# Attention over convolved features: q's tile ordered by form, then by block of n

The change makes the moving operand of an energy one piece of 1024 bytes, where it was two pieces of 512.

## Chip, cores and metric

One core of a Trainium2 chip runs the kernel. The metric is the device time of one execution in microseconds (us), lower is better; the runs of one kernel on one chip lay within 0.16% of one another here (31 of the kernel before on chip 0: 2494.62 to 2498.60 us). Kernels that are compared ran on one chip in the same rounds. Ratios are the mean time of one kernel's fast runs over that of the other's of the same rounds, so not quite the ratio of the medians that are quoted.

## The reference, cut to what matters

```python
# x: (4, 64, 64, 256) float32; Wq, Wk: 256 x 128; Wv: 256 x 256
q = einsum('bwhc,cd->bwhd', x, Wq) + bq     # k, v likewise
pq, pk, pv = (t.reshape(B, -1, N) for t in (q, k, v))          # N = 4096
energy = einsum('bcn,bcm->bnm', pq, pk)     # contraction over 128
attention = softmax(energy, axis=-1)
out = einsum('bcm,bnm->bcn', pv, attention).reshape(B, W, H, C)
return gamma * out + x
```

## The kernel before

Every float32 factor is cut into parts, so that three matmuls stand for one product: q and k each have three forms (f = 0, 1, 2). One image is 16 groups of 256 columns n; a group is 8 steps. A step makes the energies of four blocks of m, three steps ahead, and multiplies four blocks of finished weights by v. TensorE's program of a step is therefore 12 energies (sa, sa, sb, four times), then 8 matmuls with vh, 8 with vl, both into the banks `a`, and 8 with vd into `bb`. Each has a weight load of 128 columns ahead of it.

```python
def halved(f, x):
    h = f[:, :, 0, :]
    nc.scalar.activation(h, x, AF.Identity, scale=UPPER / 64)
    for j, s, op in ((1, -64.0, ALU.add), (2, 64.0 * (1.0 + E), ALU.subtract)):
        nc.vector.scalar_tensor_tensor(f[:, :, j, :], h.bitcast(F32), s, x, ALU.mult, op)

def halve_q(b, g):                                  # once in a group of 8 steps
    t = work.tile([P, NJ, 3, P], F32R, tag="q", name=f"q_{b}_{g}")     # NJ = 2
    halved(t, loads.pop((b, "qr", g)))
    loads[b, "q", g] = t

def energy(b, u, k):                                # twice in a step
    ...
    sa = ps_s.tile([P, 2, NJ, P], F32, tag="a", ...)      # one PSUM bank, of two
    sb = ps_s.tile([P, 2, NJ, P], F32, tag="b", ...)
    for i in range(2):
        for to, f, first, last in ((sa, 0, True, False), (sa, 1, False, True), (sb, 2, True, True)):
            nc.tensor.matmul(                       # out, weights (stationary), moving operand
                to[:, i], kt[:, 2 * k + i, f, :], q[:, :, f, :], start=first, stop=last
            )
    # ScalarE: exp of sa into x, then of sb into y; later VectorE: x = x*y

def attend(b, u):
    ...
    for left, right in ((h, vh), (l, vl), (d, vd)):
        for j in range(NJ):
            out_ = bb[:, j, :] if left is d else acc[j]
            for i in range(4):
                m = 2 * t + i // 2 + NI * (i % 2)
                nc.tensor.matmul(out_, left[:, i, j * P : (j + 1) * P], right[:, m, : out_.shape[1]], ...)
```

## Time and profile before

| | before |
|---|---|
| time, median of the first 3 runs | 2496.63 us (2496.11 to 2496.65) |
| TensorE, VectorE, ScalarE busy | 99%, 84%, 72% of the span |
| energies: matmuls, time from their starts to the next start | 6144, 746 us |
| granted TensorE clock | 0.999 |

The lines of the profile are shown in the prediction below. In a line of a group, the columns are the source line, the engine, the operation, output<-input, sizes and count, then the busy time in us and the mean duration of one in ns, then the engine's idle time in front. In a view by order of time, the columns are the start and the length in us and the number of instructions merged (x8). Durations of matmuls overlap (an energy's record lasts 283 ns in the mean, and the next one starts some 117 ns later), so I use the **pitch**: the time from one start to the next. Pitches to the nanosecond, in the tables, are worked out from the starts of the single records in each trace: of energies followed by an energy (and of bb followed by a matmul of attend or a transpose), with gaps of 150 ns and more, which are waits, counted apart.

### The profile page before, as it was taken

How to read it: one execution, taken by the hardware profiler on the slowest of the kernel's cores; microseconds unless marked ns; L12 is line 12 of the kernel's file. 1: busy time of each engine (PE TensorE's matmuls, PEld its weight loads, DVE VectorE, ACT ScalarE, POOL GpSimd, SP SyncE). 2: the span in 40 equal slices, each digit the busy share in tenths (PEclk: the TensorE clock that was granted, in tenths of full speed). 3: DMA queues.
4: the chain of work that ended last, by engine and by line, in shares of the span. 5: the costliest groups of instructions: out<-in, count | busy, mean ns of one | idle time of the engine just before them, and what ended most of it. 6: DMA issues, size and time to landing. Idle time of an engine off the chain costs nothing.

```text
span 2494.1 us, 50085 instructions
## 1 busy us (share of the span) xinstructions
PE 2480.4 (99%) x19982; PEld 2438.2 (98%) x19982; DVE 2106.5 (84%) x2440; ACT 1806.0 (72%) x3138; POOL 424.4 (17%) x780
## 2 busy tenths in 40 slices
PE   9999999999999999999999999999999999999998
PEld 8999999999899999999989999999998999999998
DVE  5888888888698888888869888888886988888887
ACT  5777777777677777777667777777766777777775
POOL 4211111111411111111041111111114111111110
PEclk9999999999999999999999999999999999999999
DMA  7766666665776666666477666666648666666663
GB/s 230 221 198 207 204 200 196 202 199 157 232 224 190 207 202 201 205 188 207 143 244 223 196 194 209 201 207 197 191 145 253 218 201 196 202 202 208 199 193 109
DMA packets 137408, 498.92 MB, mean 200 GB/s; under 512 B 15536, under 2 KB 57264, under 8 KB 137168
## 3 DMA queue, kind: packets, MB, share of 16 engines
q0 software_dynamic: 92320, 453.17, 58.4%
q1 hardware_dynamic: 44304, 42.22, 5.7%
q8 instruction: 160, 2.62, 0.4%
q14 instruction: 80, 0.66, 0.1%
q10 hardware_dynamic: 544, 0.26, 0.0%
HBM read 445.25 MB, written 50.33 MB: 199 GB/s over the span
## 4 chain that ended last, share of the span: by engine, by line
PE 97%; ACT 2%; DVE 1%; issue 0%; DMA 0%; SPq 0%; ACTq 0%; DVEq 0%
PE a L370 38%; PE sa L320 19%; PE bb L370 18%; PE sb L320 10%; PE qk L136 5%; PE v L157 4%; PE xt L123 1%; PE ot L416 1%; ACT h L339 1%; DVE x L334 1%; ACT x L324 0%; ACT y L324 0%; DMA x<-in_x_dram 0%; DVE vd L287 0%; ACT vh L284 0%
## 5 line engine op out<-in xcount | busy, mean ns | idle before, releaser
L324 ACT ACTIVATE x<-sa 128x512 f32<-128x512 f32 x1024 | 608.2, 594 | 400.7 <-PE sa L320 324.7
L320 PE MATMUL sa<-q,k 128*128 128x256 f32 x4096 | 757.2, 283 | 0.8 <-ACT x L324 0.8
L334 DVE TENSOR_TENSOR x<-x,y 128x1024 f32<-128x1024 f32 x512 | 625.2, 1221 | 155.6 <-ACT y L324 155.6
L320 PEld LDWEIGHTS sa<-q,k 128*128 128x128 f32 x4096 | 625.7, 189 | 2.2 <-ACT x L324 1.6
L345 DVE TENSOR_TENSOR l<-x,h 128x1024 fp32r<-128x1024 f32 x512 | 623.2, 1217 | 0.0
L348 DVE SCALAR_TENSOR_TENSOR d<-h,x 128x1024 fp32r<-128x1024 f32 x512 | 623.1, 1217 | 0.0
L324 ACT ACTIVATE y<-sb 128x512 f32<-128x512 f32 x1024 | 612.9, 599 | 0.0
L320 PE MATMUL sb<-q,k 128*128 128x256 f32 x2048 | 581.9, 284 | 0.0
L370 PE MATMUL a<-vh,h 128*128 128x258 f32 x4096 | 578.4, 284 | 0.0
L339 ACT ACTIVATE h<-x 128x1024 fp32r<-128x1024 f32 x512 | 543.3, 1061 | 42.7 <-DVE x L334 38.2
L370 PE MATMUL a<-vl,l 128*128 128x258 f32 x4096 | 573.3, 282 | 0.0
L370 PE MATMUL bb<-vd,d 128*128 128x256 f32 x4096 | 557.3, 278 | 0.0
L304 POOL DMA_DIRECT2D k<-kf x512 | 279.6, 546 | 1486.7 <-PE sb L320 1468.1
L370 PEld LDWEIGHTS a<-vh,h 128*128 128x128 f32 x4096 | 526.5, 190 | 0.0
L370 PEld LDWEIGHTS a<-vl,l 128*128 128x128 f32 x4096 | 526.2, 190 | 0.0
L370 PEld LDWEIGHTS bb<-vd,d 128*128 128x128 f32 x4096 | 514.1, 188 | 0.0
L320 PEld LDWEIGHTS sb<-q,k 128*128 128x128 f32 x2048 | 384.6, 188 | 8.9 <-ACT y L324 0.8
L136 PE MATMUL qk<-wqk_sb,xts 128*128 128x256 f32 x512 | 122.5, 382 | 0.0
L400 DVE SCALAR_TENSOR_TENSOR o<-a,o 128x256 f32<-128x256 f32 x126 | 47.6, 419 | 86.8 <-ACT o L380 86.8
L157 PE MATMUL v<-xts,wv_sb 128*128 128x256 f32 x512 | 120.3, 379 | 0.0
L157 PEld LDWEIGHTS v<-xts,wv_sb 128*128 128x128 f32 x512 | 97.3, 190 | 13.2
L408 ACT ACTIVATE o<-o,r 128x256 f32<-128x256 f32 x126 | 57.4, 502 | 72.3 <-DVE r L391 72.3
(54 smaller groups left out, 929.4 us busy)
## 6 DMA issues: line engine op xcount, KB each, us to landing
k<-kf POOLq DMA_DIRECT2D x512, 768.0 KB, 4.8
x<-in_x_dram SPq DMA_DIRECT2D x128, 256.0 KB, 3.7
kf<-f POOLq DMA_DIRECT2D x64, 384.0 KB, 4.0
out_dram<-x POOLq DMA_DIRECT2D x63, 256.0 KB, 2.5
qd<-qks POOLq DMA_DIRECT2D x128, 64.0 KB, 3.1
qr<-qd SPq DMA_DIRECT2D x64, 128.0 KB, 3.0
wv_sb<-in_L_conv_Wv_dram POOLq DMA_DIRECT2D x1, 256.0 KB, 6.2
out_dram<-x SPq DMA_DIRECT2D x1, 256.0 KB, 4.0
```

The source lines that it names most:

```text
L136: nc.tensor.matmul(qk[:, s, :], self.xt[i][:, k, s, :], wqk_sb[:, k, :], start=(k == 0), stop=(k == KC - 1),)
L157: nc.tensor.matmul(vp[:, eh, :], wv_sb[:, k, eh * P : (eh + 1) * P], self.xt[i][:, k].rearrange("p s a -> p (s a)"), start=(k == 0), stop= ...
L304: nc.gpsimd.dma_start(t.rearrange("p (i s) f d -> p i s (f d)", s=2), kf[b, u % NU])
L320: nc.tensor.matmul(to[:, i], kt[:, 2 * k + i, f, :], q[:, :, f, :], start=first, stop=last)
L324: nc.scalar.activation(to[:, 2 * k : 2 * k + 2, :], sp.rearrange("p i j d -> p i (j d)"), AF.Exp, scale=scale,)
L334: nc.vector.tensor_tensor(x, x, y, ALU.mult)
L339: nc.scalar.activation(h, units[b, u], AF.Identity, scale=UPPER)
L345: nc.vector.tensor_tensor(l, x, h.bitcast(F32), ALU.subtract)
L348: nc.vector.scalar_tensor_tensor(d, h.bitcast(F32), 1.0 + E, x, ALU.mult, ALU.subtract)
L370: nc.tensor.matmul(out_, left[:, i, j * P : (j + 1) * P], right[:, m, : out_.shape[1]], start=(t == i == 0 and (left is h or left is d and ...
L400: nc.vector.scalar_tensor_tensor(o[:, j, :], a[:, :C], 1.0 + E, o[:, j, :], ALU.mult, ALU.add)
L408: nc.scalar.activation(o[:, j, :], o[:, j, :], AF.Identity, scale=r[:, j : j + 1])
```

## The change

The intent is that the stream of an energy runs over one contiguous piece. The tile is ordered (form, block, element) in place of (block, form, element); its size, its writers and the matmuls are the same.

```diff
         def halve_q(b, g):
-            t = work.tile([P, NJ, 3, P], F32R, tag="q", name=f"q_{b}_{g}")
-            halved(t, loads.pop((b, "qr", g)))
+            t = work.tile([P, 3, NJ, P], F32R, tag="q", name=f"q_{b}_{g}")
+            halved(t.rearrange("p f j d -> p j f d"), loads.pop((b, "qr", g)))
@@ energy
-                        to[:, i], kt[:, 2 * k + i, f, :], q[:, :, f, :], start=first, stop=last
+                        to[:, i], kt[:, 2 * k + i, f, :], q[:, f], start=first, stop=last
```

## The prediction

> **What bounds the kernel now.** I read the page's busy table first, then the chain that ended last, then the groups, then the order of time of one step of the main loop, and last the records of single matmuls in the trace.
>
> ```profile
> PE 2480.4 (99%) x19982; PEld 2438.2 (98%) x19982; DVE 2106.5 (84%) x2440; ACT 1806.0 (72%) x3138; POOL 424.4 (17%) x780
> ...
> PE 97%; ACT 2%; DVE 1%; issue 0%; DMA 0%; SPq 0%; ACTq 0%; DVEq 0%
> PE a L370 38%; PE sa L320 19%; PE bb L370 18%; PE sb L320 10%; PE qk L136 5%; PE v L157 4%; PE xt L123 1%; PE ot L416 1%; ACT h L339 1%; DVE x L334 1%; ACT x L324 0%; ACT y L324 0%; DMA x<-in_x_dram 0%; DVE vd L287 0%; ACT vh L284 0%
> ```
>
> TensorE is the bound: it is 97% of the chain, and the energies (sa and sb, L320, the only matmuls that read q) are 29% of it, some 720 us. VectorE at 84% and ScalarE at 72% have slack. A busy TensorE need not run at its best rate, so what counts is the time from one matmul's start to the next, which I call pitch. The groups show that the energies are not out of line in duration:
>
> ```profile
> L320 PE MATMUL sa<-q,k 128*128 128x256 f32 x4096 | 757.2, 283 | 0.8 <-ACT x L324 0.8
> L320 PE MATMUL sb<-q,k 128*128 128x256 f32 x2048 | 581.9, 284 | 0.0
> L370 PE MATMUL a<-vl,l 128*128 128x258 f32 x4096 | 573.3, 282 | 0.0
> L370 PE MATMUL bb<-vd,d 128*128 128x256 f32 x4096 | 557.3, 278 | 0.0
> ```
>
> The bb group is the comparison to use: 256 columns too, but its moving operand vd is already one piece of 1024 bytes. An energy reads q in two pieces of 512 bytes, 1536 bytes apart. Here are a bb block and an ordinary energy block in order of time (start, length, then the instruction):
>
> ```profile
> 1005.64 1.08 PE L370 MATMUL bb<-vd,d 128*128 128x256 f32 x8
> 1006.56 0.40 PE L320 MATMUL sa<-q,k 128*128 128x256 f32 x2
> 1006.79 0.28 PE L320 MATMUL sb<-q,k 128*128 128x256 f32 x1
> ...
> 1007.85 0.28 PE L320 MATMUL sb<-q,k 128*128 128x256 f32 x1
> 1007.97 0.33 PE L370 MATMUL a<-vh,h 128*128 128x258 f32 x1
> ```
>
> Eight bb take 1006.56 - 1005.64 = 0.92 us, 115 ns each; the twelve energies take 1007.97 - 1006.56 = 1.41 us, 117.5 ns each. Now the step that follows the output transposes, once in a group of eight steps:
>
> ```profile
> 1014.80 1.11 PE L370 MATMUL bb<-vd,d 128*128 128x256 f32 x8
> 1015.75 0.40 PE L320 MATMUL sa<-q,k 128*128 128x256 f32 x2
> ...
> 1017.02 0.28 PE L320 MATMUL sb<-q,k 128*128 128x256 f32 x1
> 1017.13 0.28 PE L370 MATMUL a<-vh,h 128*128 128x258 f32 x1
> ```
>
> Here the one-piece bb need 0.95/8 = 119 ns, and the two-piece energies 1.38/12 = 115 ns: the order is reversed with nothing changed in the operands.
>
> Over the whole trace, from the starts of single matmul records (in nanoseconds, gaps over 150 left out, and those to the next kind of block): an energy's pitch has a mean of 117.4; 10% are at 113 to 115 and 83% at 117 to 119. For bb the mean is 115.9, with 55% at 113 to 115 and 24% at 117 to 119. The median record lasts 281 ns in an energy and 277 in bb. So there are **two levels, some 113.4 and some 118**, both kinds of operand reach both, and the energies sit on the upper one far more often. Sorted by the parity of the q buffer, or by the three k buffers, the energies' mean moves by 0.1 ns (all between 117.6 and 117.8 with the last of a block counted in), so addresses of buffers do not decide it.
>
> [...] in the fast level each weight load starts 3 ns after the previous matmul's start and the matmul starts 110 ns after its load, 113 in all, so the load of k seems to be the floor[...]. [...] The tenth of the energies that run at 113 to 115 with two pieces agree: the break has no fixed price.
>
> **The change part by part.**
> 1. It removes one jump in the moving operand of 64 x 8 x 12 = 6144 energies. Number of matmuls, weight loads, columns and flops stay. If the jump were all that separates the levels, each would gain at most 117.4 - 113.4 = 4.0 ns: 6144 x 4.0 = 25 us. If energies only came down to bb's mean: 6144 x (117.4 - 115.9) = 9 us. If something running beside TensorE causes the upper level, 0.
> 2. It moves where q's three forms are written: one ACTIVATE (418 ns) and two SCALAR_TENSOR_TENSOR (422 ns) per group, 64 groups. The same layout is still written for k's f tile, at the same 418 and 422 ns. All of q's halving is 64 x (0.418 + 2 x 0.422) = 81 us spread over engines with slack, and the trace has TensorE waiting on it for 0.2 us in total. A few per cent of 81 us either way stay hidden: 0.
> 3. Reading q's raw tile, the transfers and the sizes of all tiles are the same: 0 bytes added or removed, no new wait.
>
> The sum is between 0 and -25 us of 2496.63.
>
> **The rivals.** (a) *The jump costs.* For: 83% of the energies stand at 117 to 119 whatever VectorE and ScalarE are doing (means from 117.5 to 118.3 in the commonest mixes), while bb in the same mix (VectorE on x, ScalarE idle) has 113.5. Against: the block at 1015.75, and the bb at 119 there. It makes 2472 to 2488. (b) *The upper level comes from traffic beside TensorE*, or from the pace at which loads and matmuls are handed out, and contiguity is beside the point. For: the reversal, and the 258-column groups, one piece each, whose means of 119.6 and 120.1 lie 4 ns over bb[...]. It makes 2494 to 2499. (c) *The gain is made and taken back*: gaps over 150 ns in the energies already add some 24 us, nearly all in the one step of eight behind the transposes, where a PSUM bank waits for ScalarE. There a quicker energy only waits longer; it would take an eighth of any gain, and VectorE's 3 x 1.22 = 3.66 us of a 4.26 us step leaves enough slack in the other steps. (d) *A new collision* with the weight load of k or with writes by other engines, as the one-piece l and h groups may have: at +2 ns, 12 us slower.
>
> **Range and chances.** I give (b) 0.55, (a) in full or part 0.35, (d) 0.1. The weighted mean is 0.55 x 0 - 0.35 x 16 + 0.1 x 10 = -4.6; I lean a little further because of the evenness of the energies' 118: **2491 us**, with 2472 to 2501 to hold it 8 times in 10. Two per cent is 50 us, twice the most that the floor allows; a slowdown of 50 us would need +8 ns on every energy, above any mean seen here. So 0.015 faster, 0.97 the same, 0.015 slower.
>
> **What would show it.** If (a): the median energy record falls from 281 to about 277 ns, most pitches to 113 to 115, blocks of twelve take 1.37 us in place of 1.41, and the others stay. If (b): medians and shares stay, and the block behind the transposes is still the quick one. If (c): the energies are quicker but the gaps over 150 ns grow. The durations of q's three writes should stay at 418 and 422 ns within 5, and the TensorE share of the chain at 97%. I would be wrong outright if q's writes or the first energy of a group became a wait, or if a level other than these two appeared.

## The result, and the profile after

| | before | after |
|---|---|---|
| median of 4 runs | 2496.64 us | 2496.56 us |
| lowest and highest | 2496.11, 2496.82 | 2496.20, 2497.07 |
| ratio of the fast runs | | 1.000 (95%: 0.9983 to 1.0017) |
| energy: mean pitch; share at 113 to 115; at 116 to 119 | 117.38 ns; 10.3%; 87.4% | 117.39 ns; 9.8%; 88.0% |
| bb: the same | 115.90 ns; 54.8%; 32.7% | 115.90 ns; 55.2%; 31.9% |
| waits inside the energies (gaps of 150 ns and more, less 114 each) | 24.4 us | 25.5 us |

All these runs were fast ones. Nothing moved. The page of the changed kernel, its busy table and two of its groups:

```profile
PE 2481.1 (99%) x19982; PEld 2438.4 (98%) x19982; DVE 2106.9 (84%) x2440; ACT 1809.1 (73%) x3138; POOL 425.7 (17%) x780
...
L320 PE MATMUL sa<-q,k 128*128 128x256 f32 x4096 | 757.4, 283 | 1.4 <-ACT x L324 0.9
...
L320 PE MATMUL sb<-q,k 128*128 128x256 f32 x2048 | 582.0, 284 | 0.0
```

The energies' mean durations, 283 and 284 ns, are those of before to the nanosecond. The order of time shows the same two kinds of step as before, an ordinary one and the quick one, which comes once in eight steps, in the step after the one with the output transposes:

```profile
1005.39 1.08 PE L370 MATMUL bb<-vd,d 128*128 128x256 f32 x8
1006.32 0.40 PE L320 MATMUL sa<-q,k 128*128 128x256 f32 x2
...
1007.61 0.28 PE L320 MATMUL sb<-q,k 128*128 128x256 f32 x1
1007.73 1.17 PE L370 MATMUL a<-vh,h 128*128 128x258 f32 x8
...
1015.53 0.40 PE L320 MATMUL sa<-q,k 128*128 128x256 f32 x2
...
1016.80 0.28 PE L320 MATMUL sb<-q,k 128*128 128x256 f32 x1
1016.91 1.13 PE L370 MATMUL a<-vh,h 128*128 128x258 f32 x8
```

The ordinary block of twelve takes 1007.73 - 1006.32 = 1.41 us, as before; the quick one 1016.91 - 1015.53 = 1.38 us, as before. The two levels of pitch are there with one piece just as with two. The record shows more than the prediction read from it: the quick energies are not spread over the steps. In the trace before, 481 of the 557 pitches at 113 to 115 ns stand in two of the eight energy blocks of a group: the one directly behind the transposes (22% of its pitches) and the next (56%). In the six others it is 0 to 1.4%, although all eight read the same q. The changed kernel's trace has the same pattern (20%, 54%, and 0 to 1.4%). What makes those two blocks quick was not tested.

The question for the experiments was not where a gain went, since no energy became quicker, but whether pieces can cost anything at all, what does hold the energies at 118 ns, and whether anything about it can be used.

### The profile page after: what moved, and what is told of

It is laid out like the page before. It is cut to its first block, busy times and chain, and to the rows that moved or that the text cites. A ratio compares the mean times of both kernels' runs of the same rounds, so it can differ in the third digit from the quotient of the medians.

```text
span 2494.6 us, 50085 instructions
## 1 busy us (share of the span) xinstructions
PE 2481.1 (99%) x19982; PEld 2438.4 (98%) x19982; DVE 2106.9 (84%) x2440; ACT 1809.1 (73%) x3138; POOL 425.7 (17%) x780
## 3 DMA queue, kind: packets, MB, share of 16 engines
q0 software_dynamic: 92320, 453.17, 58.0%
## 4 chain that ended last, share of the span: by engine, by line
PE 95%; ACT 2%; DVE 1%; issue 1%; DMA 1%; POOL 0%; SPq 0%; ACTq 0%; DVEq 0%; POOLq 0%
PE a L370 38%; PE sa L320 19%; PE bb L370 18%; PE sb L320 10%; PE qk L136 4%; PE v L157 4%; PE ot L416 1%; PE xt L123 1%; ACT h L339 1%; DVE x L334 1%; ACT x L324 0%; ACT y L324 0%; ACT vh L284 0%; DMA kf<-f 0%; DVE vd L287 0%
```

## The experiments

All are edits of the changed kernel. "Before" in a row is the kernel before, run beside it. Where a kernel was run once (one look), the state of its run is unknown and only its trace is used in earnest. A share at 115 ns or less takes in the few pitches of 111 and 112 ns that some runs have; in the two runs at 228 ns all pitches under 400 ns are counted. The runs were made on three chips (13, 0 and 14), each with the kernel before beside it for the time. Traces of kernels that leave q and k in place agree on chips 13 and 14 (117.37 and 117.39 ns); on chip 0, where the first three shifts of address ran, no such trace was kept.

| run | time, us | before, us | ratio (95%) | energy: mean pitch, ns | at 115 or less | 120 and over | bb: mean |
|---|---|---|---|---|---|---|---|
| changed kernel | 2496.56 | 2496.64 | 1.000 (0.9983-1.0017) | 117.39 | 9.8% | 2.2% | 115.90 |
| 16-byte pieces | 2494.90 | 2495.29 | 0.9994 (0.9985-1.0003) | 116.97 | 42.6% | 23.1% | 116.69 |
| 8-byte pieces | 3161.63 | 2496.56 | 1.2664 (1.2643-1.2686) | 227.8 | 0 | 100% | 115.80 |
| single elements | 3162.04 | 2495.29 | 1.2676 (1.2655-1.2698) | 228.55 | 0 | 100% | 115.49 |
| half the columns in one of three | 2490.70 (one) | 2495.29 | | see below | | | 116.47 |
| no loads of k | 2495.11 (one) | 2495.29 | | 117.37 | 10.3% | 2.2% | 115.91 |
| no d on VectorE | 2495.76 (one) | 2496.39 | | 117.39 | 9.7% | 2.2% | (reads l) |
| q 32 bytes down | 2496.84 | 2496.56 | 1.0002 (0.9993-1.0010) | 117.70 | 15.1% | 22.0% | 115.99 |
| q 64 bytes down | 2502.59 | 2496.56 | 1.0023 (1.0014-1.0032) | 118.53 | 18.1% | 41.3% | 116.17 |
| q and k 64 bytes down | 2495.60 | 2496.56 | 0.9997 (0.9988-1.0006) | 117.01 | 19.6% | 1.7% | 116.24 |
| k 64 bytes down | 2508.12 | 2496.39 | 1.0045 (1.0028-1.0061) | 119.23 | 5.5% | 73.8% | 116.49 |
| q's pool behind k's | 2497.49 | 2496.39 | 1.0004 (0.9995-1.0013) | 117.85 | 0.1% | 2.1% | 116.05 |
| sa four times, then sb twice | **2482.80** | 2496.79 | **0.9945 (0.9932-0.9959)** | 117.33 | 11.1% | 1.7% | 115.89 |

### How small may a piece be?

The likeliest of the prediction's rivals says that a break in the operand costs nothing. A dose makes that testable: many breaks instead of one. First 64 pieces of 16 bytes.

```diff
@@ -296,4 +296,4 @@
         def halve_q(b, g):
-            t = work.tile([P, 3, NJ, P], F32R, tag="q", name=f"q_{b}_{g}")
-            halved(t.rearrange("p f j d -> p j f d"), loads.pop((b, "qr", g)))
+            t = work.tile([P, NB // 4, 3, 4], F32R, tag="q", name=f"q_{b}_{g}")
+            halved(t, loads.pop((b, "qr", g)).rearrange("p j (c e) -> p (j c) e", e=4))
             loads[b, "q", g] = t
@@ -320,3 +320,3 @@
                     nc.tensor.matmul(
-                        to[:, i], kt[:, 2 * k + i, f, :], q[:, f], start=first, stop=last
+                        to[:, i].rearrange("p j (c e) -> p (j c) e", e=4), kt[:, 2 * k + i, f, :], q[:, :, f, :], start=first, stop=last
                     )
```

> The energies' moving operand in 64 pieces of 16 bytes (48 bytes apart), results still right. Theory (the cost of an energy has nothing to do with pieces[...]): mean pitch of an energy stays at 117.4 ns within 0.3, the share at 113 to 115 ns at 10% within 2, the time at 2496.6 us within 2. Rival (a jump has a price that was too small to see for one jump): 63 jumps in place of none would be visible at even 0.2 ns each: +12 ns per energy, +75 us. The three writes of q may go up from 418 and 422 ns, hidden.

The time is 0.9994 of before's with an interval that holds 1, and q's writes stay at 417 and 421 ns. Sixty-three breaks cost nothing: at 0.2 ns each they would have cost 75 us. The spread of the energies' pitches is not untouched, which the expectation had denied: 43% now stand at 115 ns or less, but 23% at 120 and over, so the mean falls by only 0.4 ns, and bb, which does not read q, rises by 0.8 ns. The energies' total falls by 5.8 us, bb's rises by 3.9 us. The way the stream walks through memory does have an effect, but it nets to nothing.

Then single elements, 12 bytes apart, and, after that result, pieces of 8 bytes.

```diff
@@ -296,4 +296,4 @@
         def halve_q(b, g):
-            t = work.tile([P, 3, NJ, P], F32R, tag="q", name=f"q_{b}_{g}")
-            halved(t.rearrange("p f j d -> p j f d"), loads.pop((b, "qr", g)))
+            t = work.tile([P, NB // 1, 3, 1], F32R, tag="q", name=f"q_{b}_{g}")
+            halved(t, loads.pop((b, "qr", g)).rearrange("p j (c e) -> p (j c) e", e=1))
             loads[b, "q", g] = t
@@ -320,3 +320,3 @@
                     nc.tensor.matmul(
-                        to[:, i], kt[:, 2 * k + i, f, :], q[:, f], start=first, stop=last
+                        to[:, i].rearrange("p j (c e) -> p (j c) e", e=1), kt[:, 2 * k + i, f, :], q[:, :, f, :], start=first, stop=last
                     )
```

> Every element of the energies' moving operand 12 bytes from the last one, so 256 pieces of 4 bytes; results still right. Theory [...] the energy's pitch goes from 117 to over 200 ns and the time up by 500 us or more[...]. I lean to a visible slowdown of over 2%. Rival (layout is irrelevant at any size for four-byte elements): no change within 0.3 ns.

```diff
@@ -296,4 +296,4 @@
         def halve_q(b, g):
-            t = work.tile([P, 3, NJ, P], F32R, tag="q", name=f"q_{b}_{g}")
-            halved(t.rearrange("p f j d -> p j f d"), loads.pop((b, "qr", g)))
+            t = work.tile([P, NB // 2, 3, 2], F32R, tag="q", name=f"q_{b}_{g}")
+            halved(t, loads.pop((b, "qr", g)).rearrange("p j (c e) -> p (j c) e", e=2))
             loads[b, "q", g] = t
@@ -320,3 +320,3 @@
                     nc.tensor.matmul(
-                        to[:, i], kt[:, 2 * k + i, f, :], q[:, f], start=first, stop=last
+                        to[:, i].rearrange("p j (c e) -> p (j c) e", e=2), kt[:, 2 * k + i, f, :], q[:, :, f, :], start=first, stop=last
                     )
```

> The energies' moving operand in 128 pieces of 8 bytes, 24 bytes apart; results right. Before: pieces of 16 bytes cost nothing (0.9994 of the kernel before), single elements made a pitch of 228.5 ns. Theory [...]: the energies' mean stays within 2 ns of 117.4 and the time within 0.5% of 2496. Rival [...] the pitch lies between 150 and 200 ns and the kernel is 8 to 20% slower.

Here are the energies' groups by form, of the kernel with 16-byte pieces, then the one with 8-byte pieces, then the one with single elements:

```profile
L320 PE MATMUL sa<-q,k 128*128 128x256 f32 x4096 | 753.8, 281 | 0.9 <-ACT x L324 0.9
```

```profile
L320 PE MATMUL sa<-q,k 128*128 128x256 f32 x4096 | 1305.9, 410 | 0.2 <-DVE q L261 0.2
```

```profile
L320 PE MATMUL sa<-q,k 128*128 128x256 f32 x4096 | 1309.8, 410 | 0.0
```

The single elements did what I had estimated for them (over 200 ns, and 667 us more). There is a step and not a slope: 281, 410 and 410 ns. A pitch of 228 ns in place of 117 is about half the rate, and it is the same for 256 pieces of one element (228.55 ns) and 128 pieces of two (227.8 ns), so it does not count pieces. Both of my estimates for the 8-byte run missed: the mean was neither within 2 ns of 117.4 nor between 150 and 200 ns. In this kernel's float32 energies two elements in a run are too few (227.8 ns) and four are enough (116.97 ns); whether a run of three is enough was not tried. The output's pattern was split in the same way as q's, though it stays contiguous, so these runs do not show on their own that it is the reading that is slow. The original 512 bytes are 32 times the 16 that are enough.

### What a shorter stream is worth

Even if contiguity had shortened the stream, would the energies have followed? The second of the three matmuls streams half its columns here; results are wrong on purpose (they still passed the comparison, since this product is a small correction, which says nothing for them).

```diff
@@ -319,4 +319,5 @@
                 for to, f, first, last in ((sa, 0, True, False), (sa, 1, False, True), (sb, 2, True, True)):
+                    cut = slice(0, 1) if f == 1 else slice(0, NJ)
                     nc.tensor.matmul(
-                        to[:, i], kt[:, 2 * k + i, f, :], q[:, f], start=first, stop=last
+                        to[:, i, cut], kt[:, 2 * k + i, f, :], q[:, f, cut], start=first, stop=last
                     )
```

> Wrong results on purpose: the second of the three matmuls of each energy (the sa matmul that adds onto the first) streams 128 columns instead of 256, with the same weight load ahead of it. Theory A (the weight load and its hand-over to the matmul set the pitch, the stream lies under it): the time from that matmul's start to the next stays at 113 to 119 ns, at the least 108, and the kernel stays within 20 us of 2496.6. Theory B (the stream of 256 columns sets it): that interval falls towards 60 to 108 ns; if it stops at the weight load's 108 ns the kernel gains some 2048 x 9 = 18 us, if it goes to 60 ns some 115 us.

The view by order of time of this kernel, an ordinary block of twelve:

```profile
1017.90 0.34 PE L321 MATMUL sa<-q,k 128*128 128x256 f32 x2
1018.08 0.33 PE L321 MATMUL sb<-q,k 128*128 128x256 f32 x1
1018.25 0.34 PE L321 MATMUL sa<-q,k 128*128 128x256 f32 x2
...
1019.29 1.12 PE L371 MATMUL a<-vh,h 128*128 128x258 f32 x8
```

The two sa together take 0.18 us in place of 0.24, so the sb behind them starts early. Then that sb takes 0.17 us to the next start in place of 0.12. In single records, the sb starts 61 ns after the short matmul, lasts 331 ns in place of 281, and the load behind it starts 108 ns after the load before. I read this as the sb waiting for its weights. The block takes 1.39 us in place of 1.41. Over the trace the energies take 736.5 us against the changed kernel's 747.4, so each of the 2048 shortened matmuls saved 5.3 ns, although its own interval fell by over 50 (to 61 ns). Neither theory A nor B held as written: that matmul's own interval fell as in B, and the time stayed as in A, as the next took back nine tenths. Loads of energies follow one another at 108 to 109 ns at the quickest, so that here **a shorter stream gains next to nothing while every matmul has its own load**. The 113 ns level is thus close to a floor that the loads of k seem to set. It is no floor of every load: in the trace before, 66 loads of the transposes follow the one before at 95 to 103 ns.

### Is it traffic beside TensorE?

Rival (b) of the prediction put the 118 ns down to that. Two runs take away neighbours, both with wrong results on purpose: the loads of k, the largest transfers (this one failed the comparison, with a relative error of 0.32), and one of VectorE's three operations of a step (this one still passed it, which says nothing for it).

```diff
@@ -301,3 +301,5 @@
         def load_k(b, u):
-            if u < STEPS:
+            if 3 <= u < STEPS:
+                loads[b, "k", u] = loads[b, "k", u - 3]
+            elif u < STEPS:
                 t = kpool.tile([P, 4, 3, P], F32R, tag="k", name=f"k_{b}_{u}")
```

> Wrong results on purpose: k's tiles are loaded for the first three steps of an image only and used again after that, so 384 MB of transfers into SBUF and their issue on GpSimd are gone from the main loop. Theory C (the energies' upper level of 118 ns is what reading q and k costs while the transfer of the next k is being written): the share of energies at 113 to 115 ns rises from 10% to over 60%, their mean falls to under 115 ns, the kernel to under 2485 us. Rival (transfers have nothing to do with it; something on the engines or in TensorE has): the mean stays within 0.5 ns of 117.4 and the time within 5 us of 2496.6.

```diff
@@ -346,7 +346,3 @@
 
-            d = ppool.tile([P, 4, NB], F32R, tag="d", name=f"d_{b}_{u}")
-            nc.vector.scalar_tensor_tensor(
-                d, h.bitcast(F32), 1.0 + E, x, ALU.mult, ALU.subtract
-            )
-            units[b, u] = h, l, d
+            units[b, u] = h, l, l
 
@@ -365,3 +361,3 @@
                 for j in range(NJ):
-                    out_ = bb[:, j, :] if left is d else acc[j]
+                    out_ = bb[:, j, :] if right is vd else acc[j]
                     for i in range(4):
@@ -373,3 +369,3 @@
                             right[:, m, : out_.shape[1]],
-                            start=(t == i == 0 and (left is h or left is d and j == 0)),
+                            start=(t == i == 0 and (left is h or right is vd and j == 0)),
                             stop=(t == NU - 1 and i == 3 and left is not h),
```

> Wrong results on purpose: VectorE no longer makes d, and the third product reads l in its place, so VectorE works 2.44 us of a step instead of 3.66, all matmuls kept, q and k 64 bytes apart as at first. Theory E (accesses of VectorE to its tiles cause most of the upper level): the energies' share at 113 to 115 ns rises from 10% by over 20 points and the kernel gains 10 us or more. Rival (the level belongs to TensorE's two streams): share and mean of the energies within 5 points and 0.5 ns, time within 5 us, apart from shorter waits behind the transposes (up to 24 us of stalls stand there).

The first's queue line, then the second's busy table (before: 453.17 MB on that queue, and 2106.5 us on VectorE):

```profile
q0 software_dynamic: 20320, 59.92, 7.2%
```

```profile
PE 2480.1 (99%) x19982; PEld 2438.0 (98%) x19982; DVE 1539.5 (62%) x1928; ACT 1800.9 (72%) x3138; POOL 424.4 (17%) x780
```

With 393 MB of transfers gone, or 567 us of VectorE's work gone, the energies' means are 117.37 and 117.39 ns and the shares at 113 to 115 ns are 10.3% and 9.7%: the changed kernel's, to a tenth of a nanosecond. Theories C and E fell: neither the loads of k nor d's operation makes the level of 118 ns. The pattern by step stays too: the second block behind the transposes has 53% and 54% of its pitches at 113 to 115 ns, the six later ones at most 2%. ScalarE, and VectorE's other operations, were not taken away. In the trace before, the 60 pitches of energies during all of which both engines are idle have a mean of 116.7 ns, and none is at 115 or less; with the 124 at whose middle both are idle the mean is 117.9. That speaks for TensorE and what it reads, and does not show it.

### Is it the distance of q from k?

One more hint in the trace of before: of 373 places where three quick matmuls (114 ns or less) are followed by three slow ones (116 to 120), 370 are the change from bb to the first energy. What changes there is, among other things, the pair of tiles that TensorE reads, its load and its stream. (The bb block is not on one level itself: its first matmul has a mean pitch of 120.5 ns, the second 118.1, the fifth to seventh 113.9 to 114.0, and almost the same with l read in place of d. So bb's 55% is a matter of place in the block, and bb is a poor yardstick for a layout.) So the next group of runs moves the two against each other. Counted by 1024 bytes (the remainder of an address after division by 1024), q starts 64 below k in the changed kernel. What was moved to shift them is one of the kernel's pads of 64 bytes, or the small tile r.

```diff
@@ -207,4 +207,6 @@
         ppool = pool("ppool", 2)
-        pool("pad2", 1).tile([P, 16], F32, name="pad2")
-        work, kpool = pool("work", 2), pool("kpool", 3)
+        pool("pad2", 1).tile([P, 8], F32, name="pad2")
+        work = pool("work", 2)
+        pool("pad3", 1).tile([P, 8], F32, name="pad3")
+        kpool = pool("kpool", 3)
         dram = pool("dram", 2, space=DRAM)
```

> q's pool moved down by 32 bytes while k's and all pools before it stay. Theory D (the level of 118 ns is a collision inside TensorE between the weight load of k and the stream of q, which depends on their addresses' difference): the energies' share at 113 to 115 ns changes from 10% to over 40% or their mean moves by over 1 ns either way, 6 us or more. Rival (addresses do not matter, as equal means for both q buffers and all three k buffers suggest, although those are multiples of 1024 apart): share 10% within 3 points, mean 117.4 within 0.3, time within 2 us.

With 64 bytes in place of 32:

```diff
@@ -207,4 +207,5 @@
         ppool = pool("ppool", 2)
+        work = pool("work", 2)
         pool("pad2", 1).tile([P, 16], F32, name="pad2")
-        work, kpool = pool("work", 2), pool("kpool", 3)
+        kpool = pool("kpool", 3)
         dram = pool("dram", 2, space=DRAM)
```

> As the run with 32 bytes, with q moved by 64 bytes instead (q now 128 bytes before k, counted by 1024, instead of 64). Theory D: a change of the energies' share at 113 to 115 ns, not necessarily that of the 32-byte run. Rival: nothing beyond 0.3 ns and 2 us.

Both q and k moved, their distance kept:

```diff
@@ -207,3 +207,2 @@
         ppool = pool("ppool", 2)
-        pool("pad2", 1).tile([P, 16], F32, name="pad2")
         work, kpool = pool("work", 2), pool("kpool", 3)
```

> q and k both moved by 64 bytes against the tiles that VectorE and ScalarE work on, their own difference kept. Theory D (collision between q and k alone): nothing changes in the energies. Theory E (collision between TensorE's reads and the accesses of VectorE or ScalarE to their own tiles): the energies' share at 113 to 115 ns changes here, by over 10 points. If neither this nor the two other shifts changes anything, addresses are out and the level belongs to TensorE's hand-over of weights.

```diff
@@ -209,2 +209,3 @@
         work, kpool = pool("work", 2), pool("kpool", 3)
+        rpool = pool("rpool", 2)
         dram = pool("dram", 2, space=DRAM)
@@ -388,3 +389,3 @@
 
-            r = work.tile([P, 2, NJ], F32, tag="r", name=f"r_{b}_{g}")
+            r = rpool.tile([P, 2, NJ], F32, tag="r", name=f"r_{b}_{g}")
             nc.vector.reciprocal(r[:, 0, :], zall[:, b * NG + g, :])
```

> k moved down by 64 bytes with q kept, so that q and k start at the same place counted by 1024 bytes (before: q 64 below k; mean pitch of an energy 117.4 there, 117.7 at 96 below, 118.5 at 128 below). Theory D (the pitch follows the distance of q from k): a smooth trend would give 117.1 or less, 2 us; a collision at equal places could instead give over 118.5. Rival (distance does not matter and the run at 128 was a matter of q against tiles of other engines, with q now where it was at first): 117.4 within 0.2. Time within 6 us of 2496 in each.

```diff
@@ -207,4 +207,5 @@
         ppool = pool("ppool", 2)
+        kpool = pool("kpool", 3)
         pool("pad2", 1).tile([P, 16], F32, name="pad2")
-        work, kpool = pool("work", 2), pool("kpool", 3)
+        work = pool("work", 2)
         dram = pool("dram", 2, space=DRAM)
```

> The pools of k and q in the other order, with 64 bytes between them, so that q starts 64 bytes above k counted by 1024 (k moved by 128, q kept). Theory D: a mean that differs from the other four distances by over 0.3 ns in either direction; if the trend with distance is one-sided, under 117. Rival: 117.4 within 0.2. The time is to stay within 6 us of 2496.

Addresses matter, a little. The run with 32 bytes fell between its two expectations (a mean 0.3 ns higher, a share 5 points higher); the runs with q or k moved by 64 bytes refute the rival's "no change": at distances of q below k of 128, 96, 64, 0 and -64 bytes the means are 118.53, 117.70, 117.39, 119.23 and 117.85 ns, and two of the kernels are slower by more than their intervals allow for noise, by 0.23% and 0.45% (far under the 2% from which a kernel is called slower here). The energies' totals account for it: they take 752.4 us at 128 and 755.6 us at 0, against 747.4, so +5.0 and +8.2 of the 5.7 and 11.2 us that the ratios stand for; in the second, bb takes another 4.1 us. There is no trend; theory D's smooth trend (117.1 or less at distance 0) fell, and the figure that it gave for a collision (over 118.5) came true; that it is a collision is not shown. An ordinary block at distance 0 (in order of time) shows the third level, 120 ns:

```profile
1004.20 0.40 PE L321 MATMUL sa<-q,k 128*128 128x256 f32 x2
1004.44 0.28 PE L321 MATMUL sb<-q,k 128*128 128x256 f32 x1
...
1005.52 0.28 PE L321 MATMUL sb<-q,k 128*128 128x256 f32 x1
1005.64 1.13 PE L371 MATMUL a<-vh,h 128*128 128x258 f32 x8
```

1005.64 - 1004.20 = 1.44 us, 120 ns each. But the distance is not all of it, since moving both by 64 bytes with the distance kept gave 117.01 in place of 117.39 (and made bb slower by 0.3 ns, with no change in time); its share at 113 to 115 ns rose by 9.8 points, at the edge of the 10 that theory E asked for there. Nor do addresses decide alone: in that run it is the fourth block behind the transposes that is quick (74% at 113 to 115 ns) and no longer the second (0.4%), while all eight blocks still read one q. What stays open is how address and step act together, and what would bring all energies to 113 ns: none of the six placements did.

### Is it the PSUM bank?

An energy block changes banks eight times in twelve matmuls, a bb block never does. The last run makes the four sa matmuls of half a block first, then its two sb.

```diff
@@ -317,4 +317,4 @@
             sb = ps_s.tile([P, 2, NJ, P], F32, tag="b", name=f"sb_{b}_{u}_{k}")
-            for i in range(2):
-                for to, f, first, last in ((sa, 0, True, False), (sa, 1, False, True), (sb, 2, True, True)):
+            for parts in (((sa, 0, True, False), (sa, 1, False, True)), ((sb, 2, True, True),)):
+                for i, (to, f, first, last) in [(i, p) for i in range(2) for p in parts]:
                     nc.tensor.matmul(
```

> The changed kernel with the six matmuls of half an energy in another order: the four into sa, then the two into sb, so that TensorE changes the PSUM bank it writes 4 times in twelve matmuls and not 8; results right. Theory G (a change of PSUM bank between two matmuls is what holds the energies at 117 to 119 ns, as the bb matmuls, which stay in one bank, reach 113 to 115 in 55% of cases): the mean falls by over 1 ns, the share at 113 to 115 rises by over 25 points, the kernel by 6 us or more. Rival (banks have nothing to do with it): mean 117.4 within 0.4 and share 10% within 6 points; ScalarE gets sa one matmul earlier, which may shorten the 25 us of stalls behind the transposes by up to 64 x 0.1 = 6 us.

The theory fell: a mean of 117.33 ns and 11.1% at 113 to 115. And yet this kernel is **faster**, 2482.80 us against 2496.79 of the kernel before run beside it (ratio 0.9945, 0.9932 to 0.9959; under the 2% that would be called faster, but clear of noise), with right results. The gain is in the waits: those inside the energies fell from 25.5 to 10.6 us, 14.9 us. Here is the block directly behind the transposes, where most of them stand, in the changed kernel:

```profile
1011.45 0.60 ACT L324 ACTIVATE y<-sb 128x512 f32<-128x512 f32 x1
...
1011.77 0.39 PE L320 MATMUL sa<-q,k 128*128 128x256 f32 x2
...
1012.11 0.19 PEld L320 LDWEIGHTS sb<-q,k 128*128 128x128 f32 x1
1012.11 0.39 PE L320 MATMUL sb<-q,k 128*128 128x256 f32 x1
```

The sa pair at 1011.77 starts only 0.34 us before the sb; in single records of the trace before, the wait shows as a pitch of 211 ns in place of some 114, since the load of the sb starts late. ScalarE is at that time still reading the sb bank that is needed: its exp of sb ends at 1011.45 + 0.60 = 1012.05. In the new order:

```profile
1007.02 0.61 ACT L324 ACTIVATE y<-sb 128x512 f32<-128x512 f32 x1
...
1007.34 0.62 PE L320 MATMUL sa<-q,k 128*128 128x256 f32 x4
...
1007.68 0.30 PEld L320 LDWEIGHTS sb<-q,k 128*128 128x128 f32 x2
1007.79 0.39 PE L320 MATMUL sb<-q,k 128*128 128x256 f32 x2
```

ScalarE ends at 1007.63 and TensorE comes to sb's load at 1007.68 and to sb at 1007.79 on its own: two sa matmuls more lie in between, and nobody waits. Over the changed kernel's trace, this wait stands in 60 blocks behind transposes: the load of sb starts 51 ns (median) after the end of ScalarE's exp, and the pitch up to this sb is too long by 6.3 us in sum. The next pitch, sb to sa, is too long by another 6.6 us; I read this as the price of sb's load not running under a matmul. In the new order all 120 of these long pitches are gone. Of the 10.6 us that are left, 5.5 are the first pitch behind the transposes, where no exp has just ended. The expectation had allowed for up to 6 us of this, for another reason (sa ready earlier); the larger effect, sb needed later, was not foreseen.

## Why the prediction was right

Its verdict, "the same", and its range held; 2491 was 5.6 us below the measured 2496.56, since it carried a third of a chance of rival (a) and a lean beyond it.

- **What bounds the kernel.** TensorE is the bound after as before (99% busy). Its share of the chain was to stay at 97% and reads 95% in the changed kernel's page, as the chain found its way through a transfer of kf and some issue time; the time shows nothing of it.
- **Part 1, the jump: 0 to -25 us.** It is 0. The energies' mean moved by 0.01 ns. The argument from the quick tenth of the energies (two pieces at 113 to 115 ns) was sound, and 64 pieces showed it directly. That this tenth stands in two of eight blocks was not seen.
- **Part 2, the writes of q.** They stand at 418 and 422 ns, as said, and are hidden: in the changed kernel's trace the energies' matmuls wait for them for 0.5 us in total, their loads for 0.9 us.
- **Rival (a)** failed: none of its signs appeared, and 281 ns stayed 281. What the prediction said for it was misread in part. Sorted by what VectorE and ScalarE do at the middle of a pitch, the energies do not keep their mean in all mixes: in three of the nine commonest it is 116.2 to 117.2 ns, below the 117.5 to 118.3 that it gave. And the 113.5 ns of bb was that of one mix; in the other common ones bb has up to some 118.
- **Rival (b)** was right in that contiguity is beside the point, with every sign it named. Of its cause, traffic beside TensorE, the runs without k's loads and without d showed nothing; ScalarE's part and the rest of VectorE's stand untested. So the verdict came from the right half of this rival, and why the upper level exists was not known then and is not known now. The other cause it named, the pace at which loads and matmuls are handed out, was not tested on its own; that shifts of 32 and 64 bytes change the pitch speaks against pace alone. Nor are there just two levels: in the trace before, the first bb of a block already stands at 120.5 ns.
- **"Addresses of buffers do not decide it"** went too far. The buffers that it compared lie 3072 and 6144 bytes apart, both multiples of 1024; a shift of 64 bytes moves the mean by up to 1.8 ns.
- **The floor.** "The load of k seems to be the floor" was close: loads at 108 to 109 ns, and a halved stream that brings 5.3 ns of over 50.
- **Rival (c)** had no gain to take back. Its 24 us of waits were what could be had: 14.9 us of them, by another order of the matmuls. They were read too simply: 18.4 of the 24.4 us stand in the block directly behind the transposes ("nearly all"), and 12.4 of these are the wait for ScalarE. **Rival (d)** did not come about in this change, but moving k by 64 bytes cost about what it had named (11 us against 12).

## What to carry to other kernels

Before making an operand contiguous, compare it with a like operand that already is, and look for any stretch in which the piecewise one runs as fast as that: one such stretch (here the tenth of the energies at 113 to 115 ns) shows that the break has no fixed price. Sort such stretches by step and by place in the block before reading a mean as a level. Where each matmul has its own weight load, see first how closely the loads follow one another: here 108 ns against a pitch of 113 to 118, so a shorter stream could save little (5.3 ns of over 50); look at the waits between matmuls instead, and at which bank each needs next. A change of layout can also move addresses, and moving q or k by 64 bytes alone made two kernels here slower by 0.23% and 0.45%, so a difference of a few tenths of a per cent between two layouts need not be the layout's doing.
